# Loading the 7x7 convolution's banded weight rows to one half of the partitions and copying them to the other

## The chip, the cores and the metric

The program runs on one core of one Trainium2 chip. The metric is the device time of one execution in microseconds (us), from the hardware profiler, and the time quoted for a kernel is the median of several executions. The engines that matter here: the TensorE (PE, with its weight loads shown as PEld), the VectorE (DVE), the ScalarE (ACT), GpSimd (POOL) and SyncE (SP). SP and POOL both issue DMAs; the DMAs of SP run on the queue that the profile calls q1 (hardware_dynamic), those of POOL on q0 (software_dynamic), and both are served by the core's 16 DMA engines.

## The reference

An image tensor `x` of shape (8, 96, 96, 192) goes through two residual convolution blocks.

```
# layer 0
x = x + L0(gn(x))     # 192->384 product, 3x3 depthwise conv, four decaying
                      # scans (left, right, up, down), layer norm, 384->192 product
# layer 1
x = x + L1(gn(x))     # 7x7 depthwise conv + bias, layer norm over channels,
                      # 192->768 product, exact GELU, 768->192 product, times gamma
```

`gn` is a group norm with 32 groups of 6 channels over the whole image. Only the 7x7 depthwise convolution of layer 1 is touched here:

```
y = conv_general_dilated(x, dw_kernel, padding='SAME', feature_group_count=192) + dw_bias
```

Each of the 192 channels has its own 7x7 kernel, and everything is in 32-bit floats.

## The kernel before, in words

The program runs five stages, one after the other on the TensorE: A (group norm and first product, to about 778 us), B (3x3 convolution and scans, 793 to about 1835 us), C (layer norm, second product and residual, 1849 to 2868 us), D (the 7x7 convolution, 2906 to 3387 us) and E (the two products with the GELU, 3430 us to the end). Between stages, whole images go through DRAM: stage C writes the normalised-to-be image as `X1_d` and stage D writes its result as `Y_d`, which stage E reads.

**How stage D convolves.** A depthwise convolution has no sum over channels, so the TensorE is used one channel at a time. A column phase and an image row together make up the contraction rows: 63 partitions hold 21 image rows times 3 column phases (`HB = 21`, `PH = 3`). For one channel the 7x7 kernel is spread into a banded matrix, three 63x64 blocks, prepared once in stage A in DRAM as `Z2_d`: 64 rows, per channel `ZW = 208` floats. `conv_d` (line 1018) multiplies those blocks (the stationary operand, `pair[k][0]`) with the image (the moving operand, `pair[k][1]`). Two row blocks of the image lie in the two halves of the 128 partitions: `g = 0` is partitions 0 to 63, `g = 1` partitions 64 to 127. The operands of one product lie in the same partitions, so the same banded rows are wanted twice, once in each half.

**The loop.** The channels go in 32 groups of 6 (`HC = 6`). `load_d(m)` (line 740) brings group `m`: the image tile `xin` in six DMAs of 384 KB, three to each half, and the tile `band` in two DMAs of 312 KB, one to each half (64 rows of 4992 bytes). What goes to half 0 is issued by SP, what goes to half 1 by POOL. `scale_d` (line 1011) applies the group norm to `xin` in place, with eight DVE instructions. One iteration `i` of the 16 (line 1080) takes a pair of groups, `2i` and `2i+1`. In written order it does: stores of the first half of the result of iteration `i-1`, on SP (`store_d(done, i-1, 0)`); loads of groups `2i+3` and `2i+4` on both queues; stores of the second half of that result on POOL; `scale_d` for groups `2i+2` and `2i+3`; then for each of the 6 channels 72 products on the PE and four ACT instructions (line 1042) which add the bias and move PSUM to the result tile `yo`.

**What holds what.** The order on each engine is the written one (`manual_schedule`). There are five sets of `xin` and `band` (`ND = 5`), so the load of group `2i+3` waits until the PE is done with group `2i-2`, that is with iteration `i-1`. There are two `yo` tiles, so ACT can't write `yo` of iteration `i+1` before both stores of iteration `i-1` have landed. PSUM holds the products of two channels, so the PE can run two channels (144 products) ahead of ACT. A queue takes its DMAs in the order of issue, apart from small overlaps.

Group 0 is an exception: `first_d = load_d(0)` (line 985) is issued at the end of stage C, before the last stores of `X1_d`.

Of the kernel before, what the change touches and what calls it, by code (L numbers as in the profile page):

```python
# [84 lines left out]
def conv_blocks_kernel(  # L85
# [31 lines left out]
    nc = tc.nc  # L117
# [26 lines left out]
    HC = GS  # L144
# [19 lines left out]
    Z2_d = dram.tile([64, D, ZW], F32, name="Z2_d")  # L164
# [58 lines left out]
    with ExitStack() as ph:  # L223
# [247 lines left out]
        with tc.manual_schedule():  # L471
# [13 lines left out]
            for b in range(B):  # L485
                more = b + 1 < B
                for t in range(n_t):
# [28 lines left out]
                    k, j = divmod(t, NJ)  # L516
# [27 lines left out]
    with ExitStack() as ph:  # L544
# [13 lines left out]
        def load_b(k):  # L558
            c = slice(k * CC, (k + 1) * CC)
            band = bp_.tile([128, CC, 3, RB], F32, tag="band", name=f"band0_{k}")  # L560
            pin = bp_.tile([128, CC, GB, NJ, S], F32, tag="pin", name=f"pin_{k}")
            for g in range(NG):
                p = g * 64
                nc.sync.dma_start(
                    band[p : p + RB + 4].rearrange("p c t o -> p (c t o)"),
                    ZB_d[:, c].rearrange("r c t o -> r (c t o)"),
                )
                for lo, hi in ((0, RB), (RB, RB + 1), (RB + 1, RB + 2)):
                    nc.sync.dma_start(
                        pin[p + lo : p + hi].rearrange("p c b j h -> p c (b j h)"),  # L570
                        P_d[g, c, lo:hi].rearrange("c r b j h -> r c (b j h)"),
                    )
            return band, pin
# [71 lines left out]
        with tc.manual_schedule():  # L645
            loads = [load_b(k) for k in range(3)]
# [8 lines left out]
            for n in range(NI * (n_k + 1)):  # L655
                k, i = divmod(n, NI)
                z = None
                if k < n_k:
                    if i == 0:
                        band, pin = loads.pop(0)  # L660
# [79 lines left out]
    def load_d(m):  # L740
        c = m * HC
        row = D * WV * B
        pool = d_pools[m % ND > 0]
        xin = pool.tile([128, NT, BP, HC, 2 * WV], F32, tag="xin", name="xin")

        for t in range(NT):
            for g, eng in enumerate((nc.sync, nc.gpsimd)):
                src = bass.AP(
                    tensor=X1_d.tensor,
                    offset=X1_d.offset + (2 * t + g) * HG * PH * row + c * WV * B,  # L750
                    ap=[[row, 64], [1, HC * WV * B]],
                )
                eng.dma_start(
                    xin[g * 64 : (g + 1) * 64, t].rearrange("q a c n -> q (a c n)"), src
                )
        band = pool.tile([128, HC, ZW], F32, tag="band", name="band1")
        for g, eng in enumerate((nc.sync, nc.gpsimd)):
            eng.dma_start(
                band[g * 64 : (g + 1) * 64].rearrange("q c l -> q (c l)"),
                Z2_d[:, c : c + HC].rearrange("r c l -> r (c l)"),  # L760
            )
        return band, xin

    s1 = s1_pool.enter_context(tc.tile_pool(name="s1", bufs=1)).tile(
# [2 lines left out]
    with ExitStack() as ph:  # L767
# [179 lines left out]
        with tc.manual_schedule():  # L947
            load_weights()
            for u in range(n_u + 1):
# [23 lines left out]
                if held is not None:  # L973
                    k, t = divmod(u - 1, n_c)
# [8 lines left out]

            stores.pop(0)()
            first_d = load_d(0)
            for store in stores:
                store()
# [10 lines left out]
    with ExitStack() as ph:  # L998
        cp = ph.enter_context(tc.tile_pool(name="d_const", bufs=1))
        d_pools[1] = ph.enter_context(tc.tile_pool(name="d_in", bufs=ND - 1))  # L1000
        op = ph.enter_context(tc.tile_pool(name="d_out", bufs=2))
        ps_y = ph.enter_context(tc.tile_pool(name="d_ps", bufs=4, space=PSUM))

        dwb = cp.tile([128, D // CD, HC], F32, name="dwb")
        for k in range(2):
            nc.scalar.dma_start(
                dwb[k * 64 : (k + 1) * 64],
                dw_bias.rearrange("(i k c) -> k i c", k=2, c=HC)[k].partition_broadcast(64),
            )

        def scale_d(m, xin):
            xv = xin.rearrange("q t a c (v b) -> q t a c v b", b=2)
            for b in range(B):
                sc, sh = (s1[:, a, b % 2, b // 2, m : m + 1] for a in range(2))
                xw = xv[:, :, b // 2, :, :, b % 2]
                nc.vector.tensor_scalar(xw, xw, sc, sh, ALU.mult, ALU.add)  # L1016

        def conv_d(pair, c, yo, i):

            pys = [  # L1020
                [ps_y.tile([128, 2, BP, 2 * WV], F32, tag=f"py{a}", name=f"py{a}")
                 for _ in range(2)]
                for a in range(2)
            ]
            for t in range(NT):
                for n, d in enumerate((1, 0, 2)):
                    lo, hi = 2 * max(0, 1 - d), 2 * (WV - max(0, d - 1))
                    for k in range(2):
                        for g in range(2):
                            rows = slice(g * 64, g * 64 + KB)  # L1030
                            nc.tensor.matmul(  # L1031
                                pys[t // 2][g][k * 64 : (k + 1) * 64, t % 2, :, lo:hi],
                                pair[k][0][rows, c, d * ZS : d * ZS + 64],
                                pair[k][1][rows, t, :, c, lo + 2 * (d - 1) : hi + 2 * (d - 1)],
                                start=(n == 0),
                                stop=(n == 2),
                            )
                if t == 0:
                    continue
                for g in range(2):  # L1040
                    bl = slice(g, 4 + g, 2) if t == 1 else slice(4 + g, 5 + g)
                    nc.scalar.activation(
                        yo[:, bl, :, c],
                        pys[t // 2][g][:, : 2 - t // 2].rearrange("q t b (a v) -> q t (b a) v", a=NV),
                        AF.Identity,
                        bias=dwb[:, i, c : c + 1],
                        scale=1.0,
                    )

        def store_d(yo, i, k):  # L1050

            eng = (nc.sync, nc.gpsimd)[k]

            w = BP * NV * HC * 2 * WQ
            n = NV * HC * 2 * WQ if i == D // CD - 1 else w
            for at in range(0, w, n):
                for bl in range(NB):

                    pieces = [(3, HB - 3)]
                    if bl == 0:  # L1060
                        pieces.append((HB - 3, HB))
                    if bl == NB - 1:
                        pieces.append((0, 3))
                    for lo, hi in pieces:
                        r = (S - HB - bl * HG) * PH
                        src = yo[k * 64 + lo * PH : k * 64 + hi * PH, bl]
                        dst = Y_d[r + lo * PH : r + hi * PH, 2 * i + k]
                        eng.dma_start(  # L1068
                            dst.rearrange("r b a c n -> r (b a c n)")[:, at : at + n],
                            src.rearrange("r a c n -> r (a c n)")[:, at : at + n],  # L1070
                        )

        n_i = D // CD
        with tc.manual_schedule():
            loads = [first_d] + [load_d(m) for m in range(1, 3)]
            make_weights(ps_y.tile([128, 512], F32, tag="py1", name="ps_b0"))
            for m in range(2):
                scale_d(m, loads[m][1])
            done = None
            for i in range(n_i):  # L1080
                pair, loads = loads[:2], loads[2:]

                if done is not None:
                    store_d(done, i - 1, 0)
                for m in (2 * i + 3, 2 * i + 4):
                    if m < 2 * n_i:
                        loads.append(load_d(m))
                if done is not None:
                    store_d(done, i - 1, 1)
                if i + 1 < n_i:  # L1090
                    for k in range(2):
                        scale_d(2 * i + 2 + k, loads[k][1])
                done = op.tile([128, NB, BP * NV, HC, 2 * WQ], F32, tag="yo", name=f"yo_{i}")
                for c in range(HC):
                    conv_d(pair, c, done, i)
            for k in range(2):
                store_d(done, n_i - 1, k)
# [246 lines left out]
```

## Time and profile before

| what | value |
|---|---|
| median of 3 executions | 5860.17 us (5853.47 to 5860.35) |
| PE busy over the whole span | 5592.6 us, 95% |
| DVE / ACT / POOL busy over the whole span | 59% / 41% / 44% |
| share of the 16 DMA engines, stages A, B, C | 0.85, 0.91, 0.92 |
| share of the 16 DMA engines, 2890 to 3390 us (stage D) | 0.96, at 305 GB/s |
| share of the 16 DMA engines, stage E | 0.27 |
| products of stage D (line 1031) | 6912, 2906 to 3387 us |

Read it from the stage that the change is in. A share of busy time over the whole span is an average of five stages with different limits. In stage D ask three things: how busy each engine is in each stretch, what the idle stretches of the PE end with, and whether the DMA engines have time left. In a line of groups, the part ahead of the bar gives line, engine, operation, tiles and shapes; after it come total busy time, mean duration of one in ns, and the idle time ahead of them with what ended it.

### The profile page before, as it was taken

Reading aid. Unit: us, or ns where it says so; the run is one execution under the profiler, and the core shown is the slowest. Engines: PE = TensorE matmul, PEld = TensorE weight load, DVE = VectorE, ACT = ScalarE, POOL = GpSimd, SP = SyncE. Lnnn points to the kernel's source line nnn. Section 1 sums busy time; section 2 is a strip of 40 time slices with the busy share of each in tenths; the row PEclk is TensorE's granted clock in tenths of the full one; section 3 lists DMA queues with packets and bytes.
Section 4 is the critical chain, followed back from the end, with each engine's and each line's share of the span. In section 5 each row is a group of like instructions: output and inputs, shape, how many; then the busy total and the mean of one; then the engine's idle time right before and its main releaser. Section 6 shows DMA issues by size and latency. Waiting matters only on the chain.

```text
span 5860.0 us, 123059 instructions
## 1 busy us (share of the span) xinstructions
PE 5592.6 (95%) x48550; PEld 3974.4 (68%) x48550; DVE 3452.2 (59%) x8023; ACT 2426.3 (41%) x6146; POOL 2560.5 (44%) x2731
## 2 busy tenths in 40 slices
PE   6999989999998999999688869999999999999999
PEld 3655533333335999999677757777777777777777
DVE  5556459999996777777633234444444444444443
ACT  2444447777775666666344422222222222222222
POOL 1111138888886777777422223333333323333322
PEclk9999989999999999999899989999999999999999
DMA  7999879999997999999899942323222232323221
GB/s 206 275 286 257 233 202 244 243 243 243 244 244 207 268 276 282 277 282 276 255 316 327 298 120 60 80 65 81 64 68 74 64 81 65 80 65 78 63 64 40
DMA packets 634284, 1054.50 MB, mean 180 GB/s; under 512 B 108683, under 2 KB 509284, under 8 KB 633708
## 3 DMA queue, kind: packets, MB, share of 16 engines
q1 hardware_dynamic: 516924, 620.81, 40.4%
q0 software_dynamic: 110656, 423.20, 22.6%
q8 instruction: 385, 6.31, 0.5%
q10 hardware_dynamic: 6128, 2.61, 0.2%
q14 instruction: 191, 1.56, 0.1%
HBM read 585.19 MB, written 476.72 MB: 181 GB/s over the span
## 4 chain that ended last, share of the span: by engine, by line
PE 77%; DMA 6%; issue 1%; DVE 1%; SPq 1%; POOL 1%; ACT 0%; POOLq 0%; ACTq 0%; DVEq 0%
PE po L1233 19%; PE po L835 13%; PE hp L1203 13%; PE pl L582 10%; PE hp L1213 7%; PE pa L603 5%; PE pt L833 4%; DMA xin<-X_d 2%; PE pa L606 2%; PE py L1031 2%; PE pt L1186 2%; DMA Y_d<-yo 2%; DMA band<-Z_d 1%; DMA X_d<-x1c 0%; SPq L1068 0%
## 5 line engine op out<-in xcount | busy, mean ns | idle before, releaser
L1222 ACT ACTIVATE g<-hp,b0g 128x384 f32<-128x384 f32 x1152 | 563.3, 587 | 1834.3 <-PE hp L1213 1834.3
L1233 PE MATMUL po<-w1g,g 128*128 128x192 f32 x6912 | 1162.6, 327 | 0.0
L1233 PEld LDWEIGHTS po<-w1g,g 128*128 128x128 f32 x6912 | 1121.5, 190 | 1.1 <-issue 1.1
L835 PE MATMUL po<-wc,mt 128*96 128x193 f32 x4608 | 883.5, 327 | 0.0
L1190 DVE COPY yT<-pt 128x384 f32<-128x384 f32 x288 | 248.5, 863 | 1043.9 <-PE pt L1186 1043.5
L1203 PE MATMUL hp<-yT,w0w 128*128 128x384 f32 x2304 | 781.8, 489 | 0.4 <-DVE yT L1190 0.4
L1251 POOL DMA_DIRECT2D out_dram<-xo x576 | 342.6, 597 | 878.3 <-DVE xo L1240 863.5
L835 PEld LDWEIGHTS po<-wc,mt 128*96 128x96 f32 x4608 | 713.1, 164 | 3.2 <-DVE x1u L858 0.5
L582 PE MATMUL pl<-pin,band 34*32 34x380 f32 (+1 forms) x13824 | 629.8, 489 | 18.9 <-DMA pin<-P_d 18.5
L1203 PEld LDWEIGHTS hp<-yT,w0w 128*128 128x128 f32 x2304 | 429.6, 191 | 257.5 <-issue 3.7
L612 DVE TENSOR_TENSOR_SCAN z<-decay,loc 128x768 f32<-128x768 f32 x288 | 505.8, 1756 | 60.5 <-ACT loc L591 30.8
L652 POOL TENSOR_TENSOR mo<-mo,z 128x768 f32<-128x768 f32 x288 | 529.7, 1840 | 3.4 <-ACT mo L607 0.4
L29 POOL TENSOR_TENSOR rs<-rs_ve,neg_half 96x8 f32<-96x8 f32 x96 | 159.1, 1657 | 822.6 <-DVE rs_ve L28 804.6
L582 PEld LDWEIGHTS pl<-pin,band 34*32 34x32 f32 x13824 | 232.7, 107 | 397.9 <-issue 397.6
L621 DVE TENSOR_TENSOR_SCAN z<-decay,z 128x768 f32<-128x768 f32 x288 | 498.2, 1730 | 0.0
L1031 PE MATMUL py<-xin,band 63*64 63x248 f32 (+1 forms) x6912 | 406.1, 389 | 81.3 <-DVE xin L1016 50.7
L842 ACT ACTIVATE sq<-pt,mean 96x384 f32<-96x384 f32 x768 | 443.0, 577 | 25.7 <-ACT mean L839 0.8
L1031 PEld LDWEIGHTS py<-xin,band 63*64 63x64 f32 x6912 | 348.5, 140 | 138.6 <-DVE xin L1016 40.1
L603 PE MATMUL pa<-loc,mix 128*32 128x384 f32 x3456 | 431.9, 493 | 0.0
L606 PE MATMUL pa<-last,down 96*32 96x384 f32 x1152 | 426.8, 493 | 1.0 <-ACT mo L607 1.0
L1213 PE MATMUL hp<-yT,w0w 64*128 64x384 f32 x2304 | 423.5, 500 | 0.0
L365 PE MATMUL pm<-xT,win 128*128 128x384 f32 x1152 | 397.4, 496 | 5.1 <-DVE po L389 5.1
(116 smaller groups left out, 7623.8 us busy)
## 6 DMA issues: line engine op xcount, KB each, us to landing
P_d<-po POOLq DMA_DIRECT2D x96, 1152.0 KB, 9.9
pin<-P_d SPq DMA_DIRECT2D x192, 576.0 KB
mt<-M_d SPq DMA_DIRECT2D x576, 192.0 KB
xq<-in_x_dram SPq DMA_DIRECT2D x96, 576.0 KB
xr<-in_x_dram SPq DMA_DIRECT2D x384, 144.0 KB
X_d<-x1u POOLq DMA_DIRECT2D x192, 288.0 KB, 4.5
X_d<-x1c SPq DMA_DIRECT2D x192, 288.0 KB
y<-Y_d SPq DMA_DIRECT2D x24, 2304.0 KB
```

What stands on the lines that cost most here:

```text
L582: nc.tensor.matmul(pls[g][at * RB : (at + 1) * RB, :, lo:hi], band[rows, c, kh, :], pin[rows, c, :, NJ - 1 - j, lo + kh - 1 : hi + kh - 1] ...
L603: nc.tensor.matmul(pa[at], mix[:, i, at], loc[:, q], start=True, stop=True)
L606: nc.tensor.matmul(pa[at], down[:, to], last[:, q], start=True, stop=True)
L612: nc.vector.tensor_tensor_scan(zf, decay_f, loc.rearrange("p q n -> p (q n)"), 0.0, ALU.mult, ALU.add)
L621: nc.vector.tensor_tensor_scan(zr, decay_f, zr, 0.0, ALU.mult, ALU.add)
L652: nc.gpsimd.tensor_tensor(m, m, z, ALU.add)
L835: nc.tensor.matmul(po[:S, b], lhs[m], wc[:, m], start=(m == 0), stop=(m == NC - 1))
L1031: nc.tensor.matmul(pys[t // 2][g][k * 64 : (k + 1) * 64, t % 2, :, lo:hi], pair[k][0][rows, c, d * ZS : d * ZS + 64], pair[k][1][rows, t, ...
L1203: nc.tensor.matmul(hps[m, q], w0w[:, 2 * q, m * 128 : (m + 1) * 128], yT[:, 2 * q], start=True, stop=False,)
L1213: nc.tensor.matmul(hps[m, q], w0w[p, 1, m * 128 : (m + 1) * 128], yT[p, 1], start=False, stop=True,)
L1222: nc.scalar.activation(g[:, m, q], hps[m, q], AF.Gelu, bias=b0g[:, m : m + 1], scale=1.0)
L1233: nc.tensor.matmul(po[:, q], g[:, m, q, k * 128 : (k + 1) * 128], w1g[:, m], start=(m == 0), stop=(m == NE - 1),)
```

## The change

In `load_d` the band is now read from DRAM once in place of twice: for even groups into partitions 0 to 63, by SP, for odd groups into partitions 64 to 127, by POOL. In `scale_d`, ahead of the eight scaling instructions, one DVE copy of 64 partitions by 1248 floats brings the rows to the other half. Its purpose is to fetch fewer bytes. All 32 groups do so; nothing else in the program is changed.

```
         band = pool.tile([128, HC, ZW], F32, tag="band", name="band1")
-        for g, eng in enumerate((nc.sync, nc.gpsimd)):
-            eng.dma_start(
-                band[g * 64 : (g + 1) * 64].rearrange("q c l -> q (c l)"),
-                Z2_d[:, c : c + HC].rearrange("r c l -> r (c l)"),
-            )
+
+        g = m % 2
+        (nc.sync, nc.gpsimd)[g].dma_start(
+            band[g * 64 : (g + 1) * 64].rearrange("q c l -> q (c l)"),
+            Z2_d[:, c : c + HC].rearrange("r c l -> r (c l)"),
+        )
         return band, xin
...
-        def scale_d(m, xin):
+        def scale_d(m, band, xin):
+            g = m % 2
+            nc.vector.tensor_copy(
+                band[(1 - g) * 64 : (2 - g) * 64], band[g * 64 : (g + 1) * 64]
+            )
             xv = xin.rearrange("q t a c (v b) -> q t a c v b", b=2)
...
             for m in range(2):
-                scale_d(m, loads[m][1])
+                scale_d(m, *loads[m])
...
                     for k in range(2):
-                        scale_d(2 * i + 2 + k, loads[k][1])
+                        scale_d(2 * i + 2 + k, *loads[k])
```

## The prediction

> **What bounds the kernel now.** I began with the page's slices, because a share over the span hides the stages. Its rows for the DMA engines, and the PE above them:
>
> ```profile
> PE   6999989999998999999688869999999999999999
> ...
> DMA  7999879999997999999899942323222232323221
> ```
>
> Each digit is 146.5 us. Slices 21 to 23 (2930 to 3370 us) are the only ones where the PE shows 8 while the DMA engines show 9: that is stage D, the stage that the change is in. So I asked for it in 30 us stretches. Columns: stretch, length, busy us and instructions of PE, PEld, DVE, ACT, POOL, then granted clock, DMA share, GB/s.
>
> ```profile
> 3040.00:3070.00 30.00, 28.02 (x508) 24.78 (x504) 11.51 (x20) 12.29 (x24) 8.26 (x16) 0.97 1.00 339
> 3130.00:3160.00 30.00, 27.81 (x490) 23.81 (x486) 11.11 (x19) 12.61 (x24) 9.23 (x18) 0.93 1.01 348
> 3250.00:3280.00 30.00, 26.02 (x432) 20.13 (x432) 9.50 (x16) 12.29 (x24) 7.92 (x16) 0.94 1.00 317
> ```
>
> The DMA share is 0.99 to 1.01 in every stretch from 2950 to 3340 us; DVE, ACT and POOL are under half busy. Then the groups of 2890 to 3400 us, for what ends the idle time:
>
> ```profile
> L1031 PE MATMUL py<-xin,band 63*64 63x248 f32 (+1 forms) x6912 | 406.1, 389 | 81.3 <-DVE xin L1016 50.7 <-ACT yo L1042 26.6 <-issue 4.0
> L1042 ACT ACTIVATE yo<-py,dwb 128x256 f32<-128x256 f32 (+1 forms) x384 | 198.1, 581 | 320.6 <-DMA xin<-X_d 136.6 <-PE py L1031 136.4 <-DMA Y_d<-yo 47.0
> L1016 DVE TENSOR_SCALAR xin<-xin,s 128x576 f32<-128x576 f32 x256 | 152.5, 671 | 310.1 <-DMA Y_d<-yo 153.7 <-DMA xin<-X_d 112.8 <-PE py L1031 34.3
> ```
>
> The PE is idle for 81.3 us, ended by the scaling (50.7) or by ACT (26.6), and both of these in turn mostly waited for DMAs: the scaling for `xin` to arrive, ACT for the stores of `yo` to have left. Both waits are symptoms of one limit, the 16 DMA engines. The order of time shows the loop:
>
> ```profile
> 3059.31 4.85 DVE L1016 TENSOR_SCALAR xin<-xin,s 128x576 f32<-128x576 f32 x8 [15.40 <-DMA Y_d<-yo]
> 3067.25 4.78 DVE L1016 TENSOR_SCALAR xin<-xin,s 128x576 f32<-128x576 f32 x8 [3.09 <-DMA Y_d<-yo]
> 3089.04 4.74 DVE L1016 TENSOR_SCALAR xin<-xin,s 128x576 f32<-128x576 f32 x8 [17.00 <-DMA Y_d<-yo]
> ...
> 2978.76 25.93 PE L1031 MATMUL py<-xin,band 63*64 63x256 f32 x432 [3.84 <-DVE xin L1016]
> 3035.90 26.34 PE L1031 MATMUL py<-xin,band 63*64 63x256 f32 x432 [5.10 <-DVE xin L1016]
> 3064.22 7.90 PE L1031 MATMUL py<-xin,band 63*64 63x256 f32 x140 [1.98 <-DVE xin L1016]
> ...
> 3364.27 23.12 PE L1031 MATMUL py<-xin,band 63*64 63x256 f32 x428 [0.82 <-DVE xin L1016]
> ```
>
> Two scalings per iteration: the first (3059.31) is of the odd group 2i+3, and the PE starts the next iteration as it ends (3064.22); the second (3067.25) is of the even group, wanted a whole iteration later. So the odd group's arrival paces the loop. Iteration 2 starts at 2978.76, iteration 15 at 3364.27: 385.5 / 13 = **29.65 us an iteration**, where the PE by itself needs 25.9 to 26.3 for its 432 products.
>
> **What the Trainium skill says.** (1) "DMA: Bandwidth & Descriptors", section "Issuing engines are not separate DMA queues": DMAs of SP and GpSimd run on the same 16 engines and interleave. The trace agrees: by its packet records from 2950 to 3350 us both queues together fill 400.1 us of the 16 engines in 400, about half each. So bytes count, whichever queue carries them. (2) "SBUF — State Buffer", section "SBUF: two separate sides": a DVE operation in a two-port mode, which an fp32 copy from SBUF to SBUF takes, locks GpSimd out of writing DMA descriptors until it ends. No pair of rows before the change shows such a stall; it is the basis of the slower rival. (3) Price of the copy: "VectorE: DVE Perf Modes", section "The TRN2 errata", gives 58 + n/2 cycles at 0.96 GHz in that mode.
>
> **The change part by part.**
>
> *Removed: 32 band reads of 312 KB.* The DMA list of the whole run has both halves:
>
> ```profile
> band<-Z_d SPq DMA_DIRECT2D x32, 312.0 KB
> band<-Z_d POOLq DMA_DIRECT2D x32, 312.0 KB, 16.4
> ```
>
> An iteration moves twelve loads of 384 KB, four bands of 312 KB and 3456 KB of stores: 9312 KB or 9.54 MB, at 29.65 us 322 GB/s, which is the 321.8 GB/s of the packet records. Two of the four bands go: 624 KB, 6.7% of the bytes. Counted in time instead, the records give the band packets (4992 bytes, 251 ns each) 53.2 of the 400.1 us; half is 6.65%. Both say 29.65 x 0.0665 = **1.97 us an iteration**, so 27.68 us if the engines stay full. The PE's 26.3 us lie under that, so the PE doesn't take over as the bound.
>
> *Do they stay full?* Each queue loses one band of two per iteration, so neither falls behind. The tight spot is SP: it can issue the stores of iteration i only once ACT has written the last `yo`. At an iteration of 29.65 us the PE ends 4.9 + 26.3 - 29.65 = 1.6 us after the odd scaling starts, and SP's even group lands 7.9 us after it (median of the 13 gaps between the two scalings; the shortest is 6.7): 6.3 us of queued work. At 27.7 us the PE ends at 3.5, and the even group lands about 2 us (312 KB at half of 321 GB/s) sooner, at 5.9: 2.4 us queued. Refilling takes ACT's last instruction (0.6), SP's issue (0.5) and the start-up of a DMA, which I estimate at 1.8 us from the 96 KB stores of stage E (2.1 us to landing, 0.3 of it data): 2.9 us. So SP may run dry for 0.5 us in a typical iteration, 1.7 us where the gap is shortest, 1 us say on the bad side of the mean. POOL's queue then gets the engines, and only part is lost: I take half of the typical 0.5, and so **27.9 us**, a gain of 1.73. Bounds: 27.68 (nothing lost) and 28.7 (the full 1 us lost). Fourteen iterations (1 to 14) run at this pace: 14 x 1.73 = **24 us**. Iteration 0 has no stores and is PE-bound, iteration 15 has no loads.
>
> *Added: 32 copies of 64x1248.* No row shows this one. From below: (58 + 624) / 0.96 = 0.71 us by the page. The nearest rows:
>
> ```profile
> L724 DVE TENSOR_SCALAR w0w<-w0w,aff 128x768 f32<-128x768 f32 x3 | 1.7, 611 | 0.0
> L871 DVE COPY x1c<-x1u 96x768 f32<-96x768 f32 x192 | 212.5, 1107 | 6.6
> ```
>
> L724 is contiguous and takes 611 ns for 768 elements, too few for one element a cycle (800 ns), so the fast mode appears; the page's formula gives it 460, so I add the 0.15 and take 0.71 + 0.15 = **0.86 us**. From above: L871, which writes with strides, scaled to 1248 elements is 1.8 us. Two copies an iteration put 1.7 us (at most 3.6) on a DVE that is busy 9.6 of 29.65 us.
>
> *The new wait.* The copy waits for the band, and eight scalings are queued behind it on DVE, then the PE. Which band lands first? By the packet records POOL's band of an odd group ends 4 to 13 us before SP's of the same group (groups 13, 15, 29: 3083.7, 3110.9, 3323.5 against 3089.9, 3123.3, 3327.5), and SP's lands as the scaling starts. The odd group's band now comes by POOL, so its copy runs while DVE waits for SP's `xin`: hidden. The even group's comes by SP, behind its `xin`, so that scaling starts about 1 us later, hidden by the 15 to 17 us in which DVE then waits. In front of the loop it isn't hidden: group 1's band by POOL ended at 2919.5, the scaling began at 2918.38, so the first PE start moves by 1.1 + 0.86 = **2.0 us later**.
>
> *Sixteen POOL issues fewer* (0.5 us each): off the path, as POOL is mostly waiting.
>
> Sum: -24 + 2 = **-22 us, 5838 us**.
>
> **Rivals.**
> *Only part is kept* (SP runs dry for 1 us and nothing fills it, so 28.7 us): 14 x 0.95 - 2 = 11 us, 5849. For it: the reserve of 2.4 us against the 2.9 wanted. Against it: two queues keep the engines filled.
> *All of it is kept*, in the start-up too: 32 x 0.3195 MB at 0.321 MB/us = 32 us, 5828. For it: a share of 1.00. Against it: iterations 0 and 15.
> *Slower*: the loop is held by the round from the PE's end to the next arrival and not by bytes, the copy stands in front of the odd scaling (0.86), and POOL's descriptors stall behind it: 14 x 0.86 + 2 = 14 us, 5874. For it: point (2), and 0.86 us of added DVE work in the pacing chain. Against it: a share of 1.00 leaves no room for a latency bound, and POOL issues with up to several DMAs queued ahead, so that a stall of 0.9 us starves nothing.
>
> **How the numbers follow.** Forecast 0.62, part kept 0.20, all kept 0.08, slower 0.10. The forecast is the likeliest, 5838. From 5825 to 5853 are the first three cases with about 1 us an iteration of doubt on copy and queue; the slower case and some of the tails are left out, some 2 in 10. Bound of the verdict: 0.2% is 11.7 us. Faster: 0.62 and 0.08, and under half of the part-kept case, 0.78; same: the rest of it and a weak slower case, 0.13; slower 0.09.
>
> **What would show each step.** The band rows: one x16 on SP and one x16 on POOL. The copy row: x32, 64x1248, near 0.86 us. Iterations near 27.9 us between PE starts; PE idle in L1031 down from 81 to about 57 us, and a DMA share near 0.99. The odd copies start well before their scalings. The forecast is wrong if the share falls well under 0.98 while the iteration stays above 28.7 us (round-trip bound), if the odd scaling starts right behind its copy (POOL's band last), or if POOL's issues stretch beside the copies.

## The result and the profile after

The changed kernel takes 5825.6 us (median of 4 executions, 5817.3 to 5827.3) against 5860.3 for the kernel before: a ratio of 0.994, 95% interval 0.9923 to 0.9958. Measured once more beside other kernels it takes 5820.0 against 5853.6: 0.9944, interval 0.9931 to 0.9956. For this second measurement 0.9945 to 0.9952 was expected if the bytes alone count, and under 0.9935 if something else is clearly in the gain; 0.9944 lies 0.0001 below the first. The kernel is about 34 us faster where 22 were forecast: the sign was right, and the size was too small. The profile below is of an execution of 5817 us, the fastest of the first four and 8 us under their median; a second one, of 5820 us and at its median, is named beside it where a number matters.

The page's slices, PE and DMA:

```profile
PE   6999989999998999999788969999999999999999
...
DMA  7999879999997899999899842323232222323221
```

In slice 23, the last of stage D, the PE now shows 9 and the DMA engines 8. Asked for the same 330 us of stage D in one stretch (columns as in the prediction; first the kernel before, then the changed kernel, with one stretch of 30 us more):

```profile
2980.00:3310.00 330.00, 286.30 (x4884) 241.15 (x4876) 109.77 (x184) 135.73 (x264) 94.39 (x177) 0.94 1.00 324
```

```profile
2980.00:3310.00 330.00, 300.25 (x5367) 277.88 (x5363) 140.42 (x226) 155.14 (x297) 103.27 (x186) 0.96 0.99 337
3040.00:3070.00 30.00, 29.02 (x549) 28.57 (x544) 11.98 (x19) 15.57 (x31) 9.64 (x17) 1.00 0.99 329
```

5367 products in place of 4884 in the same time, at a DMA share that is still 0.99, but at 337 GB/s in place of 324. The groups of stage D:

```profile
L1036 PE MATMUL py<-xin,band 63*64 63x248 f32 (+1 forms) x6912 | 388.0, 382 | 58.4 <-DVE xin L1021 35.2 <-issue 20.4 <-DMA Y_d<-yo 2.8
L1047 ACT ACTIVATE yo<-py,dwb 128x256 f32<-128x256 f32 (+1 forms) x384 | 200.8, 577 | 277.0 <-PE py L1036 183.5 <-DMA xin<-X_d 65.7 <-DMA Y_d<-yo 27.4
L1021 DVE TENSOR_SCALAR xin<-xin,s 128x576 f32<-128x576 f32 x256 | 152.9, 678 | 118.5 <-DMA Y_d<-yo 81.5 <-DMA xin<-X_d 36.4
L1014 DVE COPY band<-band 64x1248 f32<-64x1248 f32 x32 | 25.9, 809 | 123.4 <-DMA band<-Z_d 116.6 <-PE py L1036 6.7
```

The idle time of the PE fell from 81.3 to 58.4 us (about 57 was forecast), and the waits for ACT are no longer in its line. The DVE's wait for DMAs is now split: 123.4 us in front of the copies, 118.5 in front of the scalings. The DMA list has the halved reads:

```profile
band<-Z_d SPq DMA_DIRECT2D x16, 312.0 KB
band<-Z_d POOLq DMA_DIRECT2D x16, 312.0 KB, 12.8
```

In the order of time, the odd scalings of groups 5 and 31, between them an odd group with its copy and an even one (DVE); then the PE:

```profile
2972.39 4.74 DVE L1021 TENSOR_SCALAR xin<-xin,s 128x576 f32<-128x576 f32 x8 [9.49 <-DMA Y_d<-yo]
...
3043.40 0.81 DVE L1014 COPY band<-band 64x1248 f32<-64x1248 f32 x1 [3.99 <-DMA band<-Z_d]
3051.53 4.81 DVE L1021 TENSOR_SCALAR xin<-xin,s 128x576 f32<-128x576 f32 x8 [7.33 <-DMA Y_d<-yo]
3058.87 0.80 DVE L1014 COPY band<-band 64x1248 f32<-64x1248 f32 x1 [2.53 <-DMA band<-Z_d]
3059.71 4.76 DVE L1021 TENSOR_SCALAR xin<-xin,s 128x576 f32<-128x576 f32 x8
...
3317.02 4.74 DVE L1021 TENSOR_SCALAR xin<-xin,s 128x576 f32<-128x576 f32 x8 [6.74 <-DMA Y_d<-yo]
```

```profile
2923.52 48.46 PE L1036 MATMUL py<-xin,band 63*64 63x256 f32 x864 [15.56 <-issue]
2977.18 48.91 PE L1036 MATMUL py<-xin,band 63*64 63x256 f32 x864 [5.21 <-DVE xin L1021]
3030.50 24.92 PE L1036 MATMUL py<-xin,band 63*64 63x256 f32 x432 [4.40 <-DVE xin L1021]
3056.40 23.16 PE L1036 MATMUL py<-xin,band 63*64 63x256 f32 x432 [0.98 <-DVE xin L1021]
```

The odd copy (3043.40) is over 7.33 us before its scaling starts, so it is hidden. (The profile puts that wait down to a store of `yo`; what the scaling reads is `xin`.) The even copy stands right ahead of its scaling, which nobody waits for yet. From the first of these lines to the last are 13 iterations in 344.6 us: **26.51 us** an iteration (26.70 in the second profile), where 27.9 was forecast and 29.65 measured before.

### The profile page after: what moved, and what is told of

The parts are those of the page before. It is cut to its first block, busy times and chain, and to the rows that moved or that the text cites. A ratio compares the mean times of both kernels' runs of the same rounds, so it can differ in the third digit from the quotient of the medians.

```text
span 5815.5 us, 123031 instructions
## 1 busy us (share of the span) xinstructions
PE 5571.0 (96%) x48550; PEld 3975.6 (68%) x48550; DVE 3478.3 (60%) x8055; ACT 2429.1 (42%) x6146; POOL 2556.4 (44%) x2715
## 4 chain that ended last, share of the span: by engine, by line
PE 79%; DMA 5%; DVE 1%; issue 1%; POOL 1%; SPq 0%; ACT 0%; POOLq 0%; ACTq 0%; DVEq 0%
PE po L1238 19%; PE po L836 13%; PE hp L1208 13%; PE pl L582 10%; PE hp L1218 7%; PE pa L603 5%; PE pt L834 4%; PE py L1036 3%; PE pa L606 2%; PE pt L1191 2%; DMA Y_d<-yo 2%; DMA xin<-X_d 2%; DMA band<-Z_d 1%; DVE xin L1021 0%; DMA X_d<-x1c 0%
## 5 line engine op out<-in xcount | busy, mean ns | idle before, releaser
L1036 PE MATMUL py<-xin,band 63*64 63x248 f32 (+1 forms) x6912 | 388.0, 382 | 58.4 <-DVE xin L1021 35.2
```

Of the source, the lines that this page charges most:

```text
L1036: nc.tensor.matmul(pys[t // 2][g][k * 64 : (k + 1) * 64, t % 2, :, lo:hi], pair[k][0][rows, c, d * ZS : d * ZS + 64], pair[k][1][rows, t, ...
```

## The experiments

Periods are those of the 13 iterations between the odd scalings of groups 5 and 31 in the profile of each run, rates those of the packet records from 2980 to 3300 us. Ratios are to the kernel before, run in turn with each kernel on the same chip; that kernel's own medians range from 5853.6 to 5859.1 us in the four groups of runs, so compare ratios between groups. A profile shows one execution, and not always one at the median: that of half of the band's bytes took 5806 us, 10 us under its median, and that of the odd bands by SP 5838 us, 5 us over.

| kernel | us | ratio, 95% interval | period, us | DMA share | GB/s |
|---|---|---|---|---|---|
| before (first profile) | 5860.3 | 1 | 29.66 | 1.003 | 323 |
| before, again | 5860.4 | 1.0002 (0.9994 to 1.0010) | 29.66 | 1.001 | 320 |
| changed (first profile) | 5825.6 | 0.9940 (0.9923 to 0.9958) | 26.51 | 0.995 | 336 |
| changed, again | 5820.0 | 0.9944 (0.9931 to 0.9956) | 26.70 | 0.987 | 334 |
| both reads and the copy | 5853.8 | 0.9995 (0.9987 to 1.0003) | 28.87 | 1.002 | 333 |
| both reads, other rows, and the copy | 5849.2 | 0.9990 (0.9984 to 0.9997) | 28.58 | 1.002 | 334 |
| half of the band's bytes | 5816.4 | 0.9937 (0.9923 to 0.9950) | 26.36 | 0.965 | 326 |
| all bands by SP | 5843.1 | 0.9978 (0.9969 to 0.9987) | 27.96 | 0.988 | 320 |
| odd bands by SP, even by POOL | 5833.4 | 0.9968 (0.9956 to 0.9980) | 27.89 | 0.949 | 317 |
| each copy twice | 5824.0 | 0.9949 (0.9936 to 0.9962) | 26.83 | 0.989 | 334 |
| scaling in two parts | 5816.8 | 0.9940 (0.9927 to 0.9953) | 26.59 | 1.001 | 338 |
| half of the bytes, two parts | 5800.0 | 0.9903 (0.9884 to 0.9921) | 26.04 | 0.982 | 331 |
| band first | 5818.4 | 0.9932 (0.9917 to 0.9947) | 26.51 | 0.997 | 335 |
| band first, two parts | 5811.1 | 0.9922 (0.9906 to 0.9938) | 26.25 | 1.000 | 341 |

My theory was that the bytes alone are the gain. The rivals: the copy and its wait cost or bring something of their own; the order of the queues and the chain of arrivals decide; the PE has become the bound.

**Both reads and the copy.** The copy with its wait, and all the bytes of before:

```
-        g = m % 2
-        (nc.sync, nc.gpsimd)[g].dma_start(
-            band[g * 64 : (g + 1) * 64].rearrange("q c l -> q (c l)"),
+        for g, eng in enumerate((nc.sync, nc.gpsimd)):
+            eng.dma_start(
+                band[g * 64 : (g + 1) * 64].rearrange("q c l -> q (c l)"),
...
```

> The copy of the change, with both reads of the rows kept (the copy overwrites one half with what is there already). Theory A, bytes: the DMA engines carry what they carried before, the copies are hidden behind waits, so the time is that of the kernel before plus the later first start: 5858 to 5866 us, iterations of 29 to 30 us. Rival B, the copy and its wait cost something in each iteration: about 0.85 us x 14 = 12 us or more over before, 5872 us or later. Rival C, the copy or the changed order of waits by itself brings the gain: 5826 us.

The time is that of before within its interval, so without the saved bytes there is no gain of the size seen (rival C falls), and no net cost (rival B falls), although every copy now stands straight ahead of its scaling:

```profile
3033.75 0.81 DVE L1014 COPY band<-band 64x1248 f32<-64x1248 f32 x1 [18.65 <-DMA band<-Z_d]
3034.59 4.74 DVE L1021 TENSOR_SCALAR xin<-xin,s 128x576 f32<-128x576 f32 x8
3041.37 0.80 DVE L1014 COPY band<-band 64x1248 f32<-64x1248 f32 x1 [2.04 <-DMA band<-Z_d]
3042.21 4.82 DVE L1021 TENSOR_SCALAR xin<-xin,s 128x576 f32<-128x576 f32 x8
```

An instruction in the chain that costs nothing is what full DMA engines look like. But time and period both came out below theory A's figures: the period was 28.87 us, 0.8 below before, with the same bytes moved at 333 in place of 323 GB/s. A cost of the copies that a faster DMA stream pays for can't be excluded. The granted clock does not explain that period: from 2980 to 3300 us it was 0.93 here, and 0.94 and 0.92 in the two profiles of before.

**Both reads, of other rows.** As above, but the half that is overwritten is read from other channels:

```
+            cz = c if g == m % 2 else (c + D // 2) % D
...
-                Z2_d[:, c : c + HC].rearrange("r c l -> r (c l)"),
+                Z2_d[:, cz : cz + HC].rearrange("r c l -> r (c l)"),
```

> As the run with both reads and the copy, but the half that the copy overwrites is read from rows of channels half the tensor away. As many bytes and packets, only no row is read twice at nearly the same time. Theory A, bytes: within 4 us of the run that reads the same rows twice, about 5862 us. Rival D, two reads of the same rows at nearly the same time make all packets slow, which would explain why the gain of the change (35 us) is larger than the 28 us of the bytes alone: 7 us or more below the run with the same rows, 5855 us or less, and band packets near 215 ns in place of 251.

4.6 us below the run above, with overlapping intervals (and just clear of the kernel before), and band packets of 234 ns against 236. Reading the same rows twice at nearly the same time is not what makes packets slow: rival D falls as a cause of that size; a few us of it can't be excluded.

**All bands by SP** (`g = 0` in both places).

> The changed kernel with all bands read by SP into the lower half, none by POOL. The bytes are those of the changed kernel. If only the total of bytes counts: 5825 us. If the queues have to be even (theory A with two queues that share the engines by halves): SP carries 4.77 MB an iteration as before and POOL 4.13, so SP's odd group arrives later, and a good part of the gain is lost, 5840 to 5855 us; the odd copy then stands right ahead of its scaling, which adds up to 0.85 us x 14 = 12 us.

The same bytes as the changed kernel, and only about 40% of its gain is left (2.2 thousandths of 5.6), so the total of bytes is not all that counts. The packets of SP's queue fill 0.535 of the engines, those of POOL's 0.443, and the copies are back in the chain, each right ahead of its scaling. Which of the two costs more, the uneven queues or the bare copies, this run does not separate.

**Odd bands by SP, even by POOL** (`g = 1 - m % 2` in both places).

> The changed kernel with the halves the other way round: the band of an odd group (the one that paces the loop) is read by SP, that of an even group by POOL. Bytes and balance of the queues are the same. The odd band now lands together with the last of its image rows, so that its copy stands right ahead of its scaling and is no longer hidden. Theory A, bytes: the DMA engines are full, so 0.81 us in the chain cost nothing, 5823 to 5829 us. Rival F, the round from arrival to the TensorE's start counts: 0.81 x 14 = 11 us, about 5837 us.

13.3 us slower than the changed kernel beside it (1.0 us for each of 13 iterations; the period of its profile is 1.2 us longer): rival F. Two lines show why:

```profile
3080.62 0.80 DVE L1014 COPY band<-band 64x1248 f32<-64x1248 f32 x1 [19.08 <-DMA band<-Z_d]
3081.46 4.74 DVE L1021 TENSOR_SCALAR xin<-xin,s 128x576 f32<-128x576 f32 x8
```

The odd group waits 19 us for its band, on SP's queue behind its image rows, and the copy's 0.81 us stand bare. That accounts for 0.8 us; that the rest is the 312 KB more on SP in front of the odd copy is likely, and no run has it alone. The DMA share is 0.949: the engines are not kept full, so here a latency does cost.

**Each copy twice** (the copy's instruction repeated).

> The changed kernel with each copy made twice: 0.84 us more on the VectorE per group, 1.7 us an iteration. Theory A: the odd copy lies in the wait for SP's image rows, the even one in the slack of an iteration, so only the first start moves: 0 to 2 us over the changed kernel. Rival G, the copies hold up GpSimd's descriptors or the chain: 10 us or more.

4 us above the changed kernel beside it, 5824.0 against 5820.0, with overlapping intervals; the period is 26.83 against 26.70. Of the 1.7 us that two more copies put on the VectorE in each iteration, 0.1 is seen in the period. Nothing of rival G's 10 us shows there.

**Half of the band's bytes.**

```
-            band[g * 64 : (g + 1) * 64].rearrange("q c l -> q (c l)"),
-            Z2_d[:, c : c + HC].rearrange("r c l -> r (c l)"),
+            band[g * 64 : (g + 1) * 64, : HC // 2].rearrange("q c l -> q (c l)"),
+            Z2_d[:, c : c + HC // 2].rearrange("r c l -> r (c l)"),
...
+            own = band[g * 64 : (g + 1) * 64]
+            nc.vector.tensor_copy(own[:, HC // 2 :], own[:, : HC // 2])
+            nc.vector.tensor_copy(band[(1 - g) * 64 : (2 - g) * 64], own)
```

> The changed kernel with the bytes of the band halved once more: only the rows of channels 0 to 2 of a group are read, channels 3 to 5 of the group get a copy of them (the convolution of those channels is left out in this sense; instructions on the TensorE are the same). 312 KB fewer per iteration, 3.5% of the 8.9 MB that are left. Theory A, still bound by the DMA engines: 0.035 x 26.5 to 27.5 us is 0.9 us an iteration, 12 us in all, about 5813 us. Rival E, the TensorE has become the bound: 5822 to 5827 us, and a DMA share that falls below 0.97.

0.9937 against 0.9944: no gain that can be told from none. The period is 0.15 to 0.34 us under the changed kernel's where theory A had 0.9, although the profile is of a fast execution, and the share falls to 0.965. So after the change the bytes alone are no longer the limit. The share is as rival E has it, but the PE's line still shows it waiting 37.5 us for the scaling, so the products alone are not the limit either:

```profile
L1036 PE MATMUL py<-xin,band 63*64 63x248 f32 (+1 forms) x6912 | 387.5, 383 | 54.6 <-DVE xin L1021 37.5 <-issue 17.1
```

**Scaling in two parts**, in the changed kernel:

```
-            for b in range(B):
-                ...
-                xw = xv[:, :, b // 2, :, :, b % 2]
+            for h in range(2):
+                cs = slice(h * HC // 2, (h + 1) * HC // 2)
+                for b in range(B):
+                    ...
+                    xw = xv[:, :, b // 2, cs, :, b % 2]
```

> The changed kernel with each scaling cut in two by channels: first channels 0 to 2 for all images, then 3 to 5, so that the TensorE can start on a group after half of it. If the round from arrival to start is what holds the loop now: 2 us x 14 = 28 us faster than the changed kernel at most, about 5800 us. If the DMA engines are still the bound at 336 GB/s (26.5 us for the 8.9 MB): nothing to 5 us. If it is the TensorE's own work (23 to 25 us for 432 products, by granted clock): between the two.

```profile
3073.84 6.21 DVE L1023 TENSOR_SCALAR xin<-xin,s 128x288 f32<-128x288 f32 x16 [8.92 <-DMA xin<-X_d]
3077.06 23.97 PE L1038 MATMUL py<-xin,band 63*64 63x256 f32 x432 [1.65 <-DVE xin L1023]
```

The PE does start at half of the scaling, 3.2 us after its begin in place of 4.8, and nothing comes of it (0.9940): the DMA share goes up to 1.001. The reading that fits both runs: shortening the chain alone runs into the DMA engines, taking bytes alone into the chain.

**Both together.**

> Half of the band bytes (the rows of channels 3 to 5 are copies of those of channels 0 to 2, so that the convolution of those channels is left out) and the scaling in two parts, together. Alone neither moved the time by more than its interval (ratios to before 0.9937 and 0.9940 where the changed kernel has 0.9944). Theory H, two bounds at the same place (bytes over 336 GB/s: 26.5 us; the TensorE's 23 to 25 us and the wait for the scaling: 26.4 us): together they gain 0.9 us an iteration or more, 13 us in all, about 5805 us, a ratio of 0.992. Rival E, the TensorE's products alone are the bound: 5815 us, no more than either alone.

0.9903, with an interval (0.9884 to 0.9921) that lies clear of the changed kernel's (0.9931 to 0.9956) and of that of half of the bytes (0.9923 to 0.9950): about 24 us, where each alone gave 4 us or less. The PE's idle time falls to 48.1 us. Rival E falls, and theory H's 13 us are reached. That the pair gives more than the two edits added up is not shown: the intervals of the single edits reach 10 to 12 us below the changed kernel's ratio, and in the profiles the last product ends 9.0 us earlier with half of the bytes, 4.4 with two parts and 14.6 with both than in the second profile of the changed kernel, which is close to the sum. Of these 14.6 us, 9 are 13 shorter periods (26.04 against 26.70), and 4 come from the first start (2918.3 against 2922.2 us), which half of the bytes has alone (2918.6).

**The kernel before, again.**

> The kernel before once more, for a second profile. Its first profile (5860 us) has iterations of 29.65 us at 323 GB/s, and the run with both reads and the copy has 28.9 us at 333 GB/s with the same bytes. If the first profile was a slow sample of the DMA rate: 28.8 to 29.3 us here. If the copy's place in the order makes the DMAs faster: 29.6 us again.

29.66 us and 320 GB/s: the first profile was no odd sample of the period. In these profiles the faster packets go with the kernels that have the copy. Both profiles of before are of executions above the median, by 1.5 and 3.7 us, and that part of the difference may be theirs.

**Band first**, alone and with the scaling in two parts: the block that reads the band is put ahead of the loop over the image's DMAs in `load_d`.

> The changed kernel with the band's DMA issued ahead of the image's in each group, the scaling in one part as in the changed kernel. The run with both edits has a ratio of 0.9922 to before, the scaling in two parts alone 0.9940, the changed kernel 0.9944 and 0.9940. If the order of the loads is what helps (the copies of both groups then lie in a wait, and the rows of the image land last): 0.992 to 0.993, about 5813 us. If it takes both: 0.994, about 5822 us.

> The changed kernel with the band's DMA issued ahead of the image's in each group, and the scaling in two parts. Both shorten waits and leave the bytes as they are. If the DMA engines are the bound: within 5 us of the changed kernel, 5815 to 5820 us. If waits count beside them: the even copies and the first start come 1 to 2 us earlier, 5810 us.

Alone 0.9932, nearer to what the order of the loads was to bring than to 0.994, but with an interval that holds both; with both edits 0.9922. Both lie below the changed kernel's 0.9944, with intervals that overlap its own. With both edits 5811 us came where 5810 stood for waits that count beside the bytes. Band first with two parts is the fastest version of the full computation measured, 5811 us and clearly ahead of the kernel before; that it beats the changed kernel, by 13 us going by the ratios, is likely and not shown.

## Why the prediction was right, and where it was short

**The number.** 5838 us was forecast, with a range from 5825; 5825.6 came, nearer to the rival "all of it is kept" (5828, given a chance of 0.08) than to the forecast. That it lies inside the range is in part luck. The periods of 26.5 to 26.7 us are 1 us and more under the prediction's lower bound of 27.68, and its own sum with them (14 x 3.0 to 3.15, less 2) would give 5818 to 5820 us.

**The bound.** Right. The DMA share of 1.00 was the reading that decided; the run with both reads and the copy fits it from the other side, as 0.81 us in the chain had no net cost there.

**"So bytes count, whichever queue carries them."** Wrong in its second half. With the same bytes, all bands by SP lost some 60% of the gain, and the odd bands by SP 13.3 us of it. The removed bytes are needed for the gain, as the run with both reads shows; how much of it they bring depends on the queue from which they go.

**Bytes removed: 1.97 us an iteration.** Right in kind. From both reads and the copy to the changed kernel the period falls by 28.87 - 26.51 or 26.70 = 2.2 to 2.4 us; 6.65% of 28.87 is 1.92. By the ratios (0.9995 against 0.9940 and 0.9944) that step is worth 30 to 32 us of the 34, where 14 x 1.97 are 28.

**"I take ... 27.9 us".** This is the term that was mis-sized. It wasn't so by the 0.25 us taken off because SP might run dry: at a share of 0.987 to 0.995, up to a third of a microsecond was lost, about what was allowed for. But the sum kept the rate at 322 GB/s. In the profiles it rose to 334 to 336, which by itself is 8.90 MB / 0.322 - 8.90 MB / 0.335 = 1.1 us an iteration, and explains most of 27.9 against 26.6. The run with both reads and the copy has the higher rate (333) with all the bytes, so the rise seems to come with the copies or the order of waits that they bring, not with fewer bytes. Yet by the ratios that run as a whole is only 2.9 us faster than before, and that within its interval, though its 13 periods are 10 us shorter. In its profile iteration 2 starts 1.3 and 6.9 us later than in the two profiles of before, and the last product ends 5.6 to 7.0 us earlier. How much of the 34 us is rate, and why packets become faster, stays open. The granted clock from 2980 to 3300 us also rose, from 0.94 and 0.92 to 0.96 and 0.95; whether that is cause or consequence no run separates.

**The whole time is less than the periods say.** 13 iterations x 3.0 to 3.15 us are 39 to 41 us, and the profiled executions differ by 44 us; the medians differ by 34. Of the 44 us, 3 to 5 lie behind stage D (2472.6 and 2476.4 us from the last product to the end before, 2469.7 and 2471.5 after), where nothing was changed. The profiled executions of the kernel before lay 1.5 and 3.7 us over its median, the first of the changed kernel 8 us under. The rest is likely the spread of single executions.

**The copy: 0.86 us.** 0.81 measured. The price of the Trainium skill (page "VectorE: DVE Perf Modes", section "The TRN2 errata") was 0.71; the trace decides, and the 0.15 us added from the contiguous scaling row were nearly right. The same section says that its formula comes out short of a measured copy and that the fixed term there was about 150 cycles, not 58; an estimate with that term is (150 + 624) / 0.96 = 0.81 us, which agrees with this trace.

**The new wait, hidden because POOL's band lands first.** Right, and worth more than the prediction said: the odd copies from group 5 on end 6 to 10 us before their scalings, and with the halves the other way round 13.3 us are lost.

**The first start, 2.0 us later.** Wrong in its working: band 1 by POOL ended at 2919.5 before and was taken to stay there. With band 0 and half of band 1 out of the way it ended at 2916.8 (2915.6 in the second profile), and the PE starts at 2923.5 and 2922.2, against 2923.2 and 2919.6 in the two profiles of before. A shift of 2.0 us can't be told from the 3.6 between two profiles of one kernel.

**GpSimd's descriptors behind the copies** (the slower rival, from the page "SBUF — State Buffer" of the Trainium skill, section "SBUF: two separate sides"). The prediction's sign for it, issues that stretch beside the copies, did appear. Of POOL's 152 store issues 16 overlap a copy in the changed kernel, and these took 759 ns on average, against 523 ns for all 152 before. Fifteen of them, the longest with 1105 ns among them, end 0.10 to 0.11 us after the copy that they overlap, which looks like waiting for its end; in the second profile 15 of 17 do. With half of the band's bytes, where the first copy of each pair takes only 0.48 us, issues that began 0.19 us into it took the usual 505 to 510 ns. The trace agrees with the page. The loop was not held up by it: with twice the copies the time moves by 4 us, which lies within the intervals, and the period by 0.13.

**The PE would not take over.** Right for the change, but the 25.9 to 26.3 us were no floor: the changed kernel has iterations of 23.16 us for the same 432 products, with a granted clock of 1.00. The second profile of the kernel before has one of 23.16 us too, from 2973.22, at 1.00. What made the others longer is almost all the clock: the unbroken iterations of before that took 25.93 us (from 2978.76) and 26.34 us (from 3035.90) had a granted clock of 0.90 and 0.89, and time times clock is 23.3 and 23.4 us.

## What to carry to other kernels

Where the DMA engines are full in a stage, a read that an idle engine can replace by an on-chip copy can be worth about its share of the stage's bytes, and the copy is free as long as it lies in a wait. Send what the copy needs by the queue that is ahead, not by the one whose arrival paces the loop: that choice was worth 13 of 34 us here. Once a bound has been lowered, try two edits together before giving up on each: here neither fewer bytes nor a shorter chain could be told from no gain alone, and together they brought some 24 us.

## What had not been expected of the hardware

The time of a DMA packet of one size is no constant. In the kernel before, packets of 6144 bytes took 327 ns in the stretch of stage D with loads only (2911 to 2943 us) and 300 ns among loads and stores; in the changed kernel the latter took 289 ns, at a share near 1.00 each time; those of 4992 bytes took 268, 252 and 214 ns in these three. With both reads and the copy they took 292 and 236. A sum in bytes over a rate from the trace was therefore good to some 4% only, here two thirds of the size of the effect. What sets the rate was not found.
